# A scan kernel's decays: one PSUM name with two buffers, or two names with one buffer each

## The chip, the cores and the metric

The kernel runs on one core of a Trainium2 chip. The metric is the device time of one execution in microseconds (us), lower is better. A core has five engines that run side by side, each with its own in-order queue: TensorE (PE, matmuls; its weight loads are listed as PEld), VectorE (DVE), ScalarE (ACT), GpSimd (POOL) and SyncE (SP, which here issues transfers). PSUM is the memory that TensorE writes its results to; it has eight banks of 128 partitions x 512 float32, and this kernel also uses it as fast scratch space for ScalarE and VectorE.

## The reference

The input is x of shape (2, 256, 64, 64), that is 2 batches of 256 channels by 4096 tokens. Layer 0 is a group norm and one selective scan (a Mamba block with 256 inner channels). Layer 1 is two such scans with 512 inner channels over the normalized tokens, one forward and one backward in time, and then a mixture of 8 experts of three 256 x 256 matrices each. All in float32. The heart of each of the six scans (three for each batch) is

```python
dA = jnp.exp(dt[..., None] * A)                        # decay, 16 states per channel
dBu = dt[..., None] * Bm[:, :, None, :] * xs[..., None]  # input
# h[t] = dA[t] * h[t-1] + dBu[t]
y = jnp.einsum('blds,bls->bld', hs, Cm) + xs * Dvec
y = y * jax.nn.silu(z)
return y @ out_proj_w.T
```

## The kernel before

**Tiles and loops.** Each scan is cut into 8 chunks of T = 512 tokens. A (scan, chunk) is a *step*; 48 steps run one after the other. A step with 256 inner channels has 8 *quads*, one with 512 has 16. A quad is 128 partitions x 4 groups x 512 tokens; the partitions hold 32 channels x 4 states, so that a quad is a share of the 16 states of 128 channels. There are 640 quads, numbered g. Each is worked in two *halves* h = 0 and h = 1 of two groups each; a half is a *slot*, 2g + h, of 1280 in all. The position of a quad in its run of eight is n.

**The work of one half.**
- `emit_b` (L742, GpSimd, for the whole quad, some quads ahead): the input dBu into an SBUF tile bq, from rxdt and bc.
- `emit_join` (L763, ScalarE): adds the carried state to the first token of the second group.
- `emit_decay` (L752, ScalarE, two instructions of 128 x 512): exp(dt * A) into a PSUM tile da of two banks. It calls `emit_join` first.
- `emit_scan` (L778, VectorE, 128 x 1024): the recurrence over both groups. It reads da and bq. Its result replaces da, or, where `on_pool` says so, bq.
- For a half whose result is in da: `emit_times_c` (L787, VectorE) multiplies by C into bq, and `emit_carry` (L797, ScalarE) copies the last token into h_state. For quads with n of 0, 2 or 5, and every second time for the first half of n = 4, the result goes to bq and GpSimd does both (L802, L803); then the scan is the last reader of da.
- `emit_sum` (L811, TensorE): adds over the states into y; L824 (VectorE) multiplies by the gate.

**Order.** The loop over slots writes the order of every engine out by hand: at slot s come, on ScalarE, the carry of half s-1, then the decay of half s+1, then other ScalarE work that is due; on VectorE the scan of half s, then other work, then its product with C. `in_order()` ties each engine to that order. The other work, placed by a table of slots (`SLOTS`, `Slots`), is what the next steps need: input projection, conv and its tanh (L531, L540, L544), softplus (L589 to L591 on ScalarE, L594 on VectorE, L598 on GpSimd), gates (L621, L624), norms (L399 to L431), the output projection (L841, L843, L858), and matmuls of the experts (L992, L1005) in TensorE's gaps. Behind the last slot, from about 4470 us, come the experts that found no place (L1326, L1330, L1350) and their weighting and summing (L1275, L1337, L1356).

**PSUM.** In the scan part the pools take all eight banks: `psp` three banks for projections, conv, norms and experts (L191), `ps_y` one for y, `ps_d` four for da, two tiles of two banks each (L201). Pools hand their buffers to tiles when the program is built: a tile that asks for a name (tag) gets one of the buffers of that name, and its first writer waits for the last user of the tile that had the buffer before.

Of the kernel before, what the change touches and what calls it, by code (L numbers as in the profile page):

```python
# [42 lines left out]
F32 = mybir.dt.float32  # L43
# [4 lines left out]
P = 128  # L48
NB, C, L = 2, 256, 4096
KC = C // P  # L50
T = 512
# [85 lines left out]
def hybrid_kernel(ctx: ExitStack, tc: tile.TileContext, a: dict, out: bass.AP):  # L137
    nc = tc.nc
    PSUM = bass.MemoryType.PSUM
# [54 lines left out]
    with ExitStack() as st:  # L194
# [3 lines left out]
        bcd = st.enter_context(tc.tile_pool(name="bcd", bufs=2, space=DRAM))  # L198
        bqp = st.enter_context(tc.tile_pool(name="bqp", bufs=6))
        ps_y = st.enter_context(tc.tile_pool(name="ps_y", bufs=1, space=PSUM))  # L200
        ps_d = st.enter_context(tc.tile_pool(name="ps_d", bufs=2, space=PSUM))  # L201

        lngb = const.tile([P, 2, KC], F32, name="lngb")
        one_row = const.tile([P, 1], F32, name="one_row")
# [464 lines left out]
        bq, da, y = {}, {}, {}  # L669
        pending, wanted = [], []  # L670

        def at(g):

            i, jp, n = quads[g]
            return i, 2 * jp + n // SG, n % SG
# [68 lines left out]
        def emit_decay(g, h):  # L744
            if g >= nq or ("rdt", at(g)[1]) not in cks[at(g)[0]]:
                return
            emit_join(g, h)
            i, j, sg = at(g)
            da[g, h] = ps_d.tile([P, 2, T], F32, tag="da", name=f"da_{g}_{h}")
            for k in range(2):  # L750
                q = 2 * h + k
                nc.scalar.activation(  # L752
                    da[g, h][:, k, :], cks[i]["rdt", j][:, q, :], AF.Exp,
                    scale=steps[i][0].w["a"][:, j, q * SG + sg : q * SG + sg + 1],
                )

        def emit_join(g, h):

            i, j, sg = at(g)
            job, c = steps[i]  # L760
            q = 2 * h + 1
            if c:
                nc.scalar.activation(  # L763
                    bq[g][:, q, 0:1], job.h[:, j, sg, q : q + 1], AF.Identity,
                    scale=cks[i]["a0", j][:, h, sg : sg + 1], bias=bq[g][:, q, 0:1],
                )
# [332 lines left out]
        flush(0)  # L1099
        want_b(0, 1, 2)  # L1100
        emit_decay(0, 0)

        in_order()
        done = []
        for g in range(nq):
            i, jp, n = quads[g]
            for h in range(2):
# [14 lines left out]
                if slot:  # L1122
                    emit_carry(*divmod(slot - 1, 2))
                emit_decay(*divmod(slot + 1, 2))
                sl.run(slot, "act")

# [27 lines left out]
    with ExitStack() as st:  # L1154
# [166 lines left out]
        def layer(x, l, e, tag):  # L1321
            h = mk.tile([P, KC, T], F32, tag=f"h{l}", name=f"h{l}_{tag}", bufs=2 + 2 * l)
            for m in range(KC):
                ps = psp.tile([P, T], F32, tag="ps", name=f"hp{l}_{tag}_{m}")
                for k in range(KC):
                    nc.tensor.matmul(  # L1326
                        ps, we[f"W{l + 1}", e][:, k, m * P : (m + 1) * P], x[:, k, :],
                        start=(k == 0), stop=(k == KC - 1),
                    )
                nc.scalar.activation(  # L1330
                    h[:, m, :], ps, AF.Relu,
                    bias=of[:, l, e, m : m + 1], scale=sc[:, l, e, m : m + 1],
                )
            return h
# [104 lines left out]
        for at, (b, i, e) in enumerate(pairs):  # L1439
# [5 lines left out]
            h = layer(n[b, i], 0, e, f"{i}_{e}_{b}")  # L1445
# [15 lines left out]
            while ahead and spent < target and ahead[0][2] in wb:  # L1461
                cost, fn, _ = ahead.pop(0)
# [119 lines left out]
```

## Time and profile before

| what | value |
|---|---|
| time, median of 3 runs | 5000.81 us (5000.21 to 5005.29) |
| profiled execution, its own time | 5004.36 us |
| profiled execution, span of its instructions | 5002.6 us |
| mean granted TensorE clock | 0.928 of full |
| VectorE busy in the span | 4568.5 us |
| GpSimd busy in the span | 4342.2 us |
| ScalarE busy in the span | 3617.3 us |
| TensorE busy in the span | 4256.4 us |
| decays (L752) | 2560 instructions, 686 ns each |
| scans (L778) | 1280 instructions, 2.28 to 2.35 us each |

Busy time is what an engine spent on instructions; the page also gives it as a digit (tenths) for each of 40 equal slices of the span. A row of waits reads "engine tile line <- engine tile line: us in total, times, longest us": the first waited for the second. A row of the timeline reads "start, duration, engine, line, operation, out<-in", and in brackets the idle time of the engine just before it and what ended it.

### The profile page before, as it was taken

Reading aid. Unit: us, or ns where it says so; the run is one execution under the profiler, and the core shown is the slowest. Engines: PE = TensorE matmul, PEld = TensorE weight load, DVE = VectorE, ACT = ScalarE, POOL = GpSimd, SP = SyncE. Lnnn points to the kernel's source line nnn. Section 1 sums busy time; section 2 is a strip of 40 time slices with the busy share of each in tenths; the row PEclk is TensorE's granted clock in tenths of the full one; section 3 lists DMA queues with packets and bytes.
Section 4 is the critical chain, followed back from the end, with each engine's and each line's share of the span. In section 5 each row is a group of like instructions: output and inputs, shape, how many; then the busy total and the mean of one; then the engine's idle time right before and its main releaser. Section 6 shows DMA issues by size and latency. Waiting matters only on the chain. (4 is left out here: it accounts for less than half of the span.)

```text
span 5002.6 us, 47346 instructions
## 1 busy us (share of the span) xinstructions
PE 4256.4 (85%) x14912; PEld 1473.8 (29%) x14912; DVE 4568.5 (91%) x3097; ACT 3617.3 (72%) x7304; POOL 4342.2 (87%) x1424
## 2 busy tenths in 40 slices
PE   5777778778776899989999999889868999989999
PEld 1222222222222233333333333223222333334444
DVE  6998999999999999999999999999999999964655
ACT  5777777777777788877788788888767888862232
POOL 6998999999999999999999999999999999960000
PEclk8778899999887999999999999999989999999999
DMA  5455454444444555446776555555434455436643
GB/s 192 157 188 168 157 168 153 157 144 154 163 158 148 175 179 176 166 171 232 246 238 216 171 174 169 189 171 189 169 127 146 171 185 191 171 121 236 227 160 126
DMA packets 335408, 875.26 MB, mean 175 GB/s; under 512 B 36315, under 2 KB 111861, under 8 KB 293173
## 3 DMA queue, kind: packets, MB, share of 16 engines
q1 hardware_dynamic: 326164, 835.39, 48.3%
q0 software_dynamic: 8992, 36.85, 2.8%
q8 instruction: 118, 1.93, 0.2%
q14 instruction: 134, 1.09, 0.1%
HBM read 673.27 MB, written 198.84 MB: 174 GB/s over the span
## 5 line engine op out<-in xcount | busy, mean ns | idle before, releaser
L742 POOL TENSOR_TENSOR bq<-rxdt,bc 128x2048 f32<-128x2048 f32 x640 | 2894.3, 4545 | 15.7 <-DMA rxdt<-xdtd 7.7
L752 ACT ACTIVATE da<-rdt,w_a 128x512 f32<-128x512 f32 x2560 | 1756.9, 686 | 114.2 <-DVE bq L778 68.0
L778 DVE TENSOR_TENSOR_SCAN da<-da,h_state,bq 128x1024 f32<-128x1024 f32 x664 | 1558.0, 2346 | 60.4 <-ACT da L752 46.2
L803 POOL TENSOR_TENSOR bq<-bq,bc 128x2048 f32<-128x2048 f32 (+1 forms) x280 | 1180.4, 4216 | 22.6
L778 DVE TENSOR_TENSOR_SCAN bq<-da,h_state,bq 128x1024 f32<-128x1024 f32 x456 | 1059.7, 2338 | 22.0 <-ACT da L752 21.8
L811 PE MATMUL y<-bq,stack 128*32 128x512 f32 x5120 | 744.8, 667 | 254.3 <-POOL bq L803 229.5
L787 DVE TENSOR_TENSOR bq<-da,bc 128x1024 f32<-128x1024 f32 x760 | 926.4, 1219 | 15.7
L992 PE MATMUL e<-eh,ew 128*128 128x512 f32 x1376 | 669.8, 621 | 52.3 <-DVE sp L594 13.6
L797 ACT COPY h_state<-da 128x2 f32<-128x2 f32 x759 | 119.3, 157 | 631.6 <-DVE bq L787 628.3
L763 ACT ACTIVATE bq<-h_state,bq,a 128x1 f32<-128x1 f32 x1120 | 429.8, 384 | 2.9 <-POOL bq L742 2.3
L992 PEld LDWEIGHTS e<-eh,ew 128*128 128x128 f32 x1376 | 250.5, 194 | 466.5 <-issue 234.9
L458 PE MATMUL z<-nx,w_in 128*128 128x512 f32 x640 | 326.6, 639 | 62.5 <-DVE q L423 21.1
L811 PEld LDWEIGHTS y<-bq,stack 128*32 128x32 f32 x5120 | 140.7, 116 | 798.8 <-POOL bq L803 347.7
L531 PE MATMUL conv<-xs,w_conv 64*64 64x512 f32 x2560 | 346.6, 617 | 31.3 <-ACT xs L515 29.1
L992 PE MATMUL e<-en,ew 128*128 128x512 f32 x688 | 329.6, 612 | 26.9 <-DVE xr L891 16.1
L458 PE MATMUL xs<-nx,w_in 128*128 128x512 f32 x640 | 316.9, 622 | 34.7 <-DVE sz L624 20.7
L1330 ACT ACTIVATE h<-hp,of,sc 128x512 f32<-128x512 f32 x168 | 130.6, 778 | 277.5 <-PE hp L1326 274.7
L1005 ACT ACTIVATE eh<-e,of,sc 128x512 f32<-128x512 f32 x344 | 260.1, 769 | 53.9 <-PE e L992 53.6
L843 PE MATMUL o<-sz,w_out 128*128 128x512 f32 x640 | 295.7, 601 | 0.0
L598 POOL TENSOR_TENSOR xdt<-sp,xc 128x512 f32<-128x512 f32 x160 | 203.3, 1274 | 49.7 <-DVE sp L594 49.7
L778 DVE TENSOR_TENSOR_SCAN da<-da,bq 128x1024 f32<-128x1024 f32 x96 | 219.4, 2286 | 4.3 <-ACT da L752 2.3
L458 PEld LDWEIGHTS z<-nx,w_in 128*128 128x128 f32 x640 | 123.6, 202 | 266.3 <-issue 146.8
(145 smaller groups left out, 4762.3 us busy)
## 6 DMA issues: line engine op xcount, KB each, us to landing
rxdt<-xdtd SPq DMA_DIRECT2D x160, 1024.0 KB, 6.1
rdt<-dtd SPq DMA_DIRECT2D x160, 1024.0 KB, 6.8
bc<-bcd SPq DMA_DIRECT2D x384, 256.0 KB, 3.2
ew<-in_W SPq DMA_DIRECT2D x172, 256.0 KB, 4.5
u<-u SPq DMA_DIRECT2D x86, 512.0 KB, 5.7
u<-eu SPq DMA_DIRECT2D x82, 512.0 KB, 4.1
dtd<-sp SPq DMA_DIRECT2D x160, 256.0 KB, 3.3
xdtd<-xdt SPq DMA_DIRECT2D x160, 256.0 KB, 3.5
```

The costliest lines, as they stand in the source:

```text
L458: nc.tensor.matmul(ps, job.matrices["in", half][:, k, j * P : (j + 1) * P], rhs, start=(k == 0), stop=(k == KC - 1),)
L531: nc.tensor.matmul(v[r][64 * col : 64 * col + 64, :], job.matrices["conv"][rows, 2 * jp + j, k, :], ck["xs", jp][rows, j, k : k + T] if k ...
L742: nc.gpsimd.tensor_tensor(bq[g], ck["rxdt", j], over_groups(ck["bc", 0, sg]), ALU.mult)
L752: nc.scalar.activation(da[g, h][:, k, :], cks[i]["rdt", j][:, q, :], AF.Exp, scale=steps[i][0].w["a"][:, j, q * SG + sg : q * SG + sg + 1],)
L763: nc.scalar.activation(bq[g][:, q, 0:1], job.h[:, j, sg, q : q + 1], AF.Identity, scale=cks[i]["a0", j][:, h, sg : sg + 1], bias=bq[g][:, ...
L778: nc.vector.tensor_tensor_scan(b if on_pool(g, h) else d, d, b, job.h[:, j, sg, 2 * h : 2 * h + 1] if c else 0.0, ALU.mult, ALU.add,)
L787: nc.vector.tensor_tensor(bq[g][:, two, :], d, cks[i]["bc", 1, sg].rearrange("p (o t) -> p o t", o=1).to_broadcast([P, 2, T]), ALU.mult,)
L803: nc.gpsimd.tensor_tensor(b, b, cks[i]["bc", 1, sg].rearrange("p (o t) -> p o t", o=1).to_broadcast([P, groups, T]), ALU.mult,)
L811: nc.tensor.matmul(y[i, j][q * CG : (q + 1) * CG, :], stack, bq[g][:, q, :], start=False, stop=(sg == SG - 1),)
L843: nc.tensor.matmul(v[m], job.w["out"][:, j, m * P : (m + 1) * P], ck["sz", j], start=False, stop=(j == job.nj - 1),)
L992: nc.tensor.matmul(ps, ew[l][:, k, m * P : (m + 1) * P], key[x][:, k, :], start=(k == 0), stop=(k == KC - 1),)
L1005: nc.scalar.activation(key[dst][:, m, :], key["ps", l, m], AF.Relu, bias=of[:, l, e, m : m + 1], scale=sc[:, l, e, m : m + 1],)
```

## The change

The pool of the decays gets one buffer for each name in place of two, and the two halves of a quad get names of their own, da0 and da1. Each name has one pair of banks; the pool keeps four banks. First halves then always lie in one pair and second halves in the other.

```diff
-        ps_d = st.enter_context(tc.tile_pool(name="ps_d", bufs=2, space=PSUM))
+        ps_d = st.enter_context(tc.tile_pool(name="ps_d", bufs=1, space=PSUM))
...
-            da[g, h] = ps_d.tile([P, 2, T], F32, tag="da", name=f"da_{g}_{h}")
+            da[g, h] = ps_d.tile([P, 2, T], F32, tag=f"da{h}", name=f"da_{g}_{h}")
```

## The prediction

> **What bounds the kernel now.** I read the page's busy rows and slices first, then the waits of each engine between 60 and 4467 us (first to last scan), then the timeline around single decays.
>
> ```profile
> PE 4256.4 (85%) x14912; PEld 1473.8 (29%) x14912; DVE 4568.5 (91%) x3097; ACT 3617.3 (72%) x7304; POOL 4342.2 (87%) x1424
> DVE  6998999999999999999999999999999999964655
> POOL 6998999999999999999999999999999999960000
> ```
>
> From the second to about the 36th slice (to some 4470 us) the scans run, and there VectorE and GpSimd are both at 9 tenths; ScalarE never is. The rest (533 us) is expert matmuls behind the scans. By stretch (columns: us, PE, PEld, DVE, ACT, POOL busy with counts, clock, DMA share, GB/s):
>
> ```profile
> 1000.00:1500.00 500.00, 394.25 (x1559) 119.72 (x1552) 482.92 (x331) 379.84 (x797) 485.78 (x160) 0.90 0.46 154
> 1500.00:2000.00 500.00, 424.12 (x1569) 141.27 (x1568) 491.81 (x320) 390.91 (x808) 497.34 (x161) 0.93 0.49 170
> 2000.00:2500.00 500.00, 458.68 (x1505) 166.29 (x1503) 478.96 (x288) 398.45 (x802) 489.18 (x149) 0.96 0.58 203
> ```
>
> Neither leads everywhere. In the first and third row both leave 10 to 21 us idle; in the second GpSimd leaves 2.7 us and VectorE 8.2. Who waits for whom (us, times, longest; 60 to 4467 us):
>
> ```profile
> DVE da L778 <- ACT da L752: 48.4, 55, 3.9
> DVE bq L778 <- ACT da L752: 26.3, 22, 2.2
> DVE da L778 <- POOL h_state L802: 2.6, 3, 1.6
> DVE da L778 <- POOL bq L742: 1.2, 1, 1.2
> POOL h_state L802 <- DVE bq L778: 53.3, 37, 5.7
> ACT da L752 <- DVE bq L778: 68.0, 80, 2.0
> ```
>
> VectorE's largest idle time, 74.7 us, is scans waiting for their decays. For GpSimd it waits about 4 us in all; GpSimd waits 53.3 us for its scans. So VectorE mostly sets the pace with GpSimd close behind, and decays cost it 74.7 us. The last row is the change's subject: 80 decays waited for a scan of the kind that leaves its result in bq. Which scan? Here is one (start, duration, engine, line):
>
> ```profile
> 1054.35 1.21 DVE L787 TENSOR_TENSOR bq<-da,bc 128x1024 f32<-128x1024 f32 x1
> 1055.48 2.34 DVE L778 TENSOR_TENSOR_SCAN bq<-da,h_state,bq 128x1024 f32<-128x1024 f32 x1
> 1057.74 0.67 DVE L594 SCALAR_TENSOR_TENSOR sp<-dt,sp 128x512 f32<-128x512 f32 x1
> 1059.30 2.36 DVE L778 TENSOR_TENSOR_SCAN da<-da,h_state,bq 128x1024 f32<-128x1024 f32 x1 [0.90 <-ACT da L752]
> ```
>
> and ScalarE beside it:
>
> ```profile
> 1055.81 0.14 ACT L797 COPY h_state<-da 128x2 f32<-128x2 f32 x1
> 1055.85 0.39 ACT L763 ACTIVATE bq<-h_state,bq,a 128x1 f32<-128x1 f32 x1
> 1057.85 1.42 ACT L752 ACTIVATE da<-rdt,w_a 128x512 f32<-128x512 f32 x2 [1.62 <-DVE bq L778]
> ```
>
> The decay at 1057.85 feeds the scan at 1059.30. The half two before it was finished with its banks at 1055.95 (the carry copy, L797), yet the decay stood until 1057.82, where the scan of the half *just before* ended. Nothing but a da pair is shared by those two instructions. So the two pairs do not strictly alternate: this half was given its neighbour's pair while the other stood empty.
>
> **The change part by part.** It adds and removes no instruction, transfer or bank: ps_d stays at four banks, two pairs. The order on every engine is the program's own. Decays are emitted h = 0, 1, 0, 1, so with a pair for each h, half s can only wait for half s-2, never for s-1.
>
> *The waits that go.* Following all 1280 decay pairs through the timeline, I count 31 that start within 0.15 us of the end of the immediately preceding scan and whose idle time that scan ended: 43.4 us of ScalarE. (The other waits of the 80 end with the scan two back, as they must, and stay.) What VectorE loses is the idle time ahead of the decay's scan. In 11 of the 31 it is 1.48 us (two decays of 0.69 and the hand-over), in 13 it is 0.90 (one 0.67 us instruction stood between), in one 0.81, and in six nothing, as filler covered it. Sum: 11 x 1.48 + 13 x 0.90 + 0.81 = 28.8 us.
>
> After the change, the decay of the example could start at about 1056.2, behind its join (L763), and end near 1057.6. The softplus step (L594) ends at 1058.41 and the scan would follow. ScalarE's work behind the decay (L589 to L591) moves up by 1.6 us as well; what is late next on VectorE is then nothing but its own queue.
>
> *What is added.* Behind a half that took its neighbour's pair, the next half used to find a pair idle since three halves back; now it waits for the one two back. That costs ScalarE nothing new, because it has already passed the same scan in its own order. I put it at 0. Its bounds: 0, and in each of the 31 places the hand-over seen above between the scan's end and the decay, 0.03 us, together 1 us. Queued behind such a decay on ScalarE would be the evictions of conv, z and the experts, for which PE and VectorE wait.
>
> *A rule of the Trainium skill.* The row: a 0.90 us bubble in every step from 716 to 1398 us, at the same place. Perfetto Trace Analysis, section Optimization Strategy, says that a gap repeating on the engine that should be saturated can mean too little SBUF or PSUM for the next tile, and it names buffer count and tile size. By that reading this change would bring 0, as it adds no bank, and a third pair would be wanted. The trace goes the other way: a pair was empty from 1055.95 while the decay waited. What lacked was the choice, not the count. I side with the trace.
>
> *How much of the 28.8 us reaches the end.* A gain of VectorE counts only where GpSimd was waiting for VectorE afterwards; where GpSimd runs without a wait, it absorbs the gain. From the waits in order of time (GpSimd's at L802 and L598):
> - 60 to 500 us: five gaps, 4.5 us; GpSimd waits about 13 us. Some of this stretch is limited at job changes by PE and ScalarE (3.5 us on thx at 441): I count 3.4.
> - 500 to 1500: seven gaps, 6.3 us; a step of 113 us has about 0.97 + 0.98 us of GpSimd waits, enough for 0.90, but also 0.2 and 0.63 us of VectorE waiting for the conv's tanh, which may grow: 5.0.
> - 1500 to 2220: 0.90 + 1.48. GpSimd waits nowhere between 1487 and 2277, and at 2220.88 VectorE waits 1.19 us for GpSimd: 0.
> - 2220 to 2830: five of 1.48 and one of 0.81, 8.2 us; GpSimd waits some 19 us, but VectorE also has waits of 2.9, 2.7 and 3.9 us for late decays that have other causes: 6.5.
> - 2830 to 3560: 1.48 at 3508, followed by GpSimd waits of 0.69 and 1.48: 1.5.
> - 3560 to 4400: 1.48 at 3832, no GpSimd wait until 4429: 0.
> - 4400 to 4460: three of 1.48; GpSimd then waits 5.7 us: 4.4.
>
> Sum 20.8 us. Behind it, PE's sum of the last quad (L811 at 4468.14) follows the last scan and PE runs without a gap until 4494, so the tail moves with it. Against the profiled execution (5004.36 us, of which 1.8 lie outside its span of 5002.6) that is 4983.6; against the median of the runs, 5000.81, it is 4980.0, the number I give.
>
> **The rivals.**
> *The gain is absorbed.* GpSimd is 97 to 99% busy; if it is the true pace-maker in more than the two stretches, only the places directly ahead of its waits count. For it: the 1500 to 2000 row. Against it: 53.3 us of waits for scans. With the last stretch (4.4), half of the fourth (3.3) and 1.5, it is 9 us: 4992. Should the pairs alternate already, so that the change does nothing, it is 5001; the example speaks against it.
>
> *More comes back.* ScalarE gets 43.4 us of standing back, and other late decays (74.7 - 28.8 = 45.9 us) have a late ScalarE behind them. All 28.8 and a quarter of 45.9: 40 us, 4961.
>
> *Slower: other banks are dealt anew.* The mechanism that dealt da pairs badly also deals the three banks of psp (L191) and the three th buffers, by when tiles are held to be free. If the releases of da move, those choices may move too. A bad choice there makes PE wait for an eviction, then ScalarE for PE, then a decay is late. The price is that of the nearest row, 0.90 us on VectorE for each. It decides where more than 23 new ones lie on the path (20.8 / 0.90). With one in each of the 48 steps, 43 us are lost and 21 won: +22, 5023. Against it: the order of each engine is fixed and PE has 41 to 106 us idle in the three stretches shown.
>
> **How the numbers follow.** The likeliest case, most of the gain (4972 to 4990), has 0.60. More coming back has 0.12, absorbed or nothing 0.21, newly dealt banks 0.07. About 0.2% (10 us) is what a measurement of this kernel can tell from no change. Absorbed splits around 4991, so that faster by over 0.2% gets 0.60 + 0.12 + 0.03 = 0.75, within 0.2% 0.18, and slower by more 0.07. For the range I leave out the outer half of more coming back (0.06), newly dealt banks (0.07) and the part of absorbed in which nothing at all is won (0.06), 0.19 together: 4965 to 5000.
>
> **What would show it.** In the changed profile: ScalarE's wait of da for DVE bq L778 falls from 68.0 us to about 25, and each such wait that is left ends with a scan two halves back; scans waiting for decays fall from 74.7 to about 46; GpSimd's wait for scans falls by some 20 us; instructions stay at 47346 but for semaphores; the last scan starts near 4444 in place of 4465. It is wrong if decays still wait for the scan just before them, or if these waits go and the last scan stays: then GpSimd set the pace and VectorE's idle time has only changed its name. New waits of PE or ScalarE in rows of conv, e or thx would be the slower case.

## The result, and the profile after

The changed kernel takes 4978.36 us (median of 5, 4972.65 to 4982.88), the kernel before 5000.21 us (median of 5). The ratio is 0.9954, 95% interval [0.9939, 0.9968]: 22 us or somewhat under half a percent faster, twice what the measurement can tell from no change. The forecast was 4980.0, range 4965 to 5000.

The profiled execution of the changed kernel took 4972.65 us, its span 4970.9 us. It is 5.7 us below its median, and the one of before was some 4 us above, so the pair of traces shows 31.7 us where the medians show 22. Of the 31.7 the scans account for 27.8: the last scan starts at 4437.4 us in place of 4465.2. The rest behind it took 533.5 us in place of 537.4. In the other traces below that rest took 533 or 537 to 540 us without any edit to it, so these 3.9 us are not the change's.

The page's busy row: the work is the same to 0.1% on VectorE, ScalarE and GpSimd, and the number of instructions has not changed. TensorE is busy 30.6 us less, at a mean granted clock of 0.933 in place of 0.928; E7 shows a part of it.

```profile
PE 4225.8 (85%) x14912; PEld 1476.1 (30%) x14912; DVE 4567.6 (92%) x3097; ACT 3613.1 (73%) x7304; POOL 4340.4 (87%) x1424
```

Who waits for whom, 60 to 4467 us (us, times, longest):

```profile
DVE da L778 <- ACT da L752: 35.7, 52, 4.9
DVE bq L778 <- ACT da L752: 9.3, 10, 2.2
DVE da L778 <- POOL h_state L802: 4.3, 4, 1.6
POOL h_state L802 <- DVE bq L778: 36.0, 29, 3.1
ACT da L752 <- DVE bq L778: 23.6, 48, 1.4
ACT nx L493 <- DMA x<-in_x: 20.6, 7, 4.2
```

Scans waiting for decays: 74.7 us before, 45.0 now (46 forecast). Decays waiting for a scan: 68.0 before, 23.6 now (25 forecast), and followed one by one through the trace none of these waits ends with the scan just before it; there were 31 such. GpSimd's wait for scans: 53.3 to 36.0. The last row is new: it was 8.6 us, see E4.

The same half as in the prediction's example, first VectorE, then ScalarE:

```profile
1050.28 2.34 DVE L778 TENSOR_TENSOR_SCAN bq<-da,h_state,bq 128x1024 f32<-128x1024 f32 x1
1052.53 0.66 DVE L594 SCALAR_TENSOR_TENSOR sp<-dt,sp 128x512 f32<-128x512 f32 x1
1053.11 2.35 DVE L778 TENSOR_TENSOR_SCAN da<-da,h_state,bq 128x1024 f32<-128x1024 f32 x1
```

```profile
1050.61 0.14 ACT L797 COPY h_state<-da 128x2 f32<-128x2 f32 x1
1050.65 0.39 ACT L763 ACTIVATE bq<-h_state,bq,a 128x1 f32<-128x1 f32 x1
1050.94 1.40 ACT L752 ACTIVATE da<-rdt,w_a 128x512 f32<-128x512 f32 x2
```

The decay at 1050.94 follows its join at once and runs beside the scan that it used to wait for (1050.28 to 1052.62). The scan at 1053.11 follows softplus without a gap; the 0.90 us are gone.

Was anything else dealt anew? The two programs have the same instructions in the same order on every engine. Only decays differ in what they wait for, and no tile but the decays' lies at another place. In the program of before, 37 of the 1280 halves have their neighbour's pair: the 31 that were seen to wait, and six whose decay came late enough. In the changed program none has.

How much earlier the same scan starts in the changed trace gives the gain by stretch:

| stretch of before (us) | forecast gain | measured gain |
|---|---|---|
| 60 to 526 | 3.4 | 0.5 |
| 526 to 1481 | 5.0 | 7.6 |
| 1481 to 2235 | 0 | -0.8 |
| 2235 to 2836 | 6.5 | 11.7 |
| 2836 to 3548 | 1.5 | 0.9 |
| 3548 to 4409 | 0 | 0.7 |
| 4409 to the last scan | 4.4 | 7.2 |
| sum | 20.8 | 27.8 |

The second row is the least certain. In a second trace of the changed kernel (E11) the second scan, 526 us to about 1430, took 897.5 us against 893.2 in the first and 901.3 in the kernel before. So up to 4 us there, and of single scans in that part or behind 2240 us, can belong to the execution and not to an edit; E11's last scan is 1.8 us later than the first trace's, which would make the sum 26. The sum is of the right size, yet most of its terms are off. The experiments ask why.

### The profile page after: what moved, and what is told of

The parts are those of the page before. It is cut to its first block, busy times and chain, and to the rows that moved or that the text cites. A ratio compares the mean times of both kernels' runs of the same rounds, so it can differ in the third digit from the quotient of the medians.

```text
span 4970.9 us, 47346 instructions
## 1 busy us (share of the span) xinstructions
PE 4225.8 (85%) x14912; PEld 1476.1 (30%) x14912; DVE 4567.6 (92%) x3097; ACT 3613.1 (73%) x7304; POOL 4340.4 (87%) x1424
## 5 line engine op out<-in xcount | busy, mean ns | idle before, releaser
L742 POOL TENSOR_TENSOR bq<-rxdt,bc 128x2048 f32<-128x2048 f32 x640 | 2893.8, 4544 | 15.2 <-DMA rxdt<-xdtd 7.3
L752 ACT ACTIVATE da<-rdt,w_a 128x512 f32<-128x512 f32 x2560 | 1756.9, 686 | 70.0 <-DVE bq L778 23.6
L787 DVE TENSOR_TENSOR bq<-da,bc 128x1024 f32<-128x1024 f32 x760 | 926.2, 1219 | 15.7
L992 PE MATMUL e<-eh,ew 128*128 128x512 f32 x1376 | 659.5, 613 | 43.3 <-DVE sp L594 14.4
L531 PE MATMUL conv<-xs,w_conv 64*64 64x512 f32 x2560 | 334.6, 603 | 22.7 <-ACT xs L515 20.4
```

Of the source, the lines that this page charges most:

```text
L531: nc.tensor.matmul(v[r][64 * col : 64 * col + 64, :], job.matrices["conv"][rows, 2 * jp + j, k, :], ck["xs", jp][rows, j, k : k + T] if k ...
L742: nc.gpsimd.tensor_tensor(bq[g], ck["rxdt", j], over_groups(ck["bc", 0, sg]), ALU.mult)
L752: nc.scalar.activation(da[g, h][:, k, :], cks[i]["rdt", j][:, q, :], AF.Exp, scale=steps[i][0].w["a"][:, j, q * SG + sg : q * SG + sg + 1],)
L787: nc.vector.tensor_tensor(bq[g][:, two, :], d, cks[i]["bc", 1, sg].rearrange("p (o t) -> p o t", o=1).to_broadcast([P, 2, T]), ALU.mult,)
L992: nc.tensor.matmul(ps, ew[l][:, k, m * P : (m + 1) * P], key[x][:, k, :], start=(k == 0), stop=(k == KC - 1),)
```

## The experiments

Most of them name the pair by a table in the changed kernel. A half in `shared` gets its neighbour's pair, all others alternate. The table adds four lines, so that decays are L756 and scans L782 there.

```diff
+        pair = [0]
+        for slot in range(1, 2 * nq):
+            pair.append(pair[-1] if slot in shared else 1 - pair[-1])
...
-            da[g, h] = ps_d.tile([P, 2, T], F32, tag=f"da{h}", name=f"da_{g}_{h}")
+            da[g, h] = ps_d.tile([P, 2, T], F32, tag=f"da{pair[2 * g + h]}", name=f"da_{g}_{h}")
```

"Later by" below is the start of a scan in the experiment's trace less that of the same scan in the changed kernel's.

**E1: 13 shared pairs where GpSimd has no waits.**

```diff
+        shared = {437 + 32 * k for k in range(6)} | {1045 + 32 * k for k in range(7)}
```

> The changed kernel, with the pair of banks of each half named by a table: all halves alternate, but 13 (the second half of the second n = 2 quad of a step, whose neighbour leaves its result in bq) are given their neighbour's pair, six between 1500 and 2150 us and seven between 3600 and 4350 us, where the changed kernel's GpSimd has no waits for scans. Theory A (a wrong choice of pair costs VectorE its idle time, and GpSimd's own pace absorbs it here): each of the 13 decays waits for the scan just before it, 1.48 us of idle VectorE each, 19 us in all, but the last scan starts within 5 us of the changed kernel's 4437 us, and the time is 4975 to 4985 us. Rival B (every idle microsecond of VectorE is on the path): the last scan starts near 4456 and the time is about 4997 us.

Measured: 4988.43 us, ratio to before 0.9977 [0.9969, 0.9985]. All 13 decays wait for the scan just before them, and each leaves VectorE 1.48 us idle. One of them:

```profile
1925.32 2.35 DVE L782 TENSOR_TENSOR_SCAN bq<-da,h_state,bq 128x1024 f32<-128x1024 f32 x1 [1.48 <-ACT da L756]
```

The last scan starts 15.3 us late (4452.7; 13.5 against E11's trace), 10 us more than theory A allowed. The first pair of each set (1597 and 3658 us) costs nothing: within some 60 us, waits that VectorE has in the changed kernel are shorter by as much. The five pairs that follow in the third scan raise the delay from 1.85 us at 1689 us to 3.44, 4.69, 5.66, 6.86 and 7.96 us at 2175 us: 1.0 to 1.6 each, and nothing comes back within the step. At 2220 us 2.2 us do come back, in a wait of 2.16 us that the changed kernel has there anyway; 3.2 us are lost anew from 2235 to 2280 us, where no pair is shared (1.7 of them at a wait like the last one of E7). Busy time from 1600 to 2190 us in the changed kernel, then in E1 (columns as in the prediction):

```profile
1600.00:2190.00 590.00, 526.29 (x1916) 182.67 (x1920) 583.33 (x379) 477.48 (x986) 586.86 (x189) 0.97 0.51 179
```

```profile
1600.00:2190.00 590.00, 528.58 (x1903) 179.18 (x1902) 578.66 (x377) 476.91 (x985) 583.30 (x186) 0.95 0.49 176
```

GpSimd's idle time grows from 3.1 to 6.7 us. It set the pace there, but with VectorE so close behind that it absorbs only some 0.3 us of each 1.48 of these five. Neither A nor B holds as written; B is nearer.

**E2: 13 shared pairs where GpSimd waits.**

```diff
+        shared = {149 + 32 * k for k in range(7)} | {629} | {645 + 16 * k for k in range(5)}
```

> The same table, with the 13 shared pairs where the changed kernel's GpSimd waits for scans: seven between 590 and 1300 us (one in each step of the second scan), six between 2240 and 2520 us. Theory A: the 19 us of VectorE's idle time come through but for what lies beside other waits, the last scan starts 13 to 19 us later than 4437 us and the time is 4990 to 4998 us. Rival B: the same 19 us, as in the other place. Rival C (the gain of the change came from something else than the shared pairs): no difference in either, 4978 us.

Measured: 4988.50 us, 0.9978 [0.9971, 0.9985]; the last scan 14.7 us late. The seven of the second scan cost 11.5 us against the first trace of the changed kernel, some 7 against E11's (1.0 to 1.6 each), the six behind 2240 us 4.7 us (0.8 each). In the time there is no difference between E1's place and this one. So C falls, 13 shared pairs in either place bring back half of the 22 us; and the map of GpSimd's waits alone, by which the prediction weighed each stretch, is no guide to the price.

**E3: 240 shared pairs.**

```diff
+        shared = {16 * k + n for k in range(nq // 8) for n in (1, 5, 11)}
```

> The same table, with every second half of an n = 0, 2 or 5 quad in its neighbour's pair: 240 of 1280 instead of the 31 that were seen to wait before the change. Theory A: up to 1.48 us each, 355 us, less what GpSimd's pace and filler absorb, some 20 to 100 us: 5230 to 5310 us. A lower price, below 0.5 us each (under 5100 us), would mean that the decay is seldom on the path and that the gain of 22 us is owed to a few places only.

Measured: 5333.79 us, 1.0673 [1.0657, 1.0689], above the expected band. Totals of waits of ScalarE and of GpSimd:

```profile
ACT da L756 <- DVE bq L782: 420.7, 248, 2.7
```

```profile
POOL h_state L806 <- DVE bq L782: 341.3, 118, 6.9
```

231 of the 240 decays are seen to wait for the scan just before them. VectorE's gaps at their scans are 242 us, but the last scan starts 363 us late: 1.5 us for each shared pair, half as much again as the gaps at their own scans. What the rest is made of was not isolated; TensorE's mean granted clock is 0.91 here, and 0.93 in the changed kernel.

**E4: the scaling of x one slot later.** After the change ScalarE stands 20.6 us at L493 for a transfer, since it is earlier and the transfer is not.

```diff
-AHEAD_SLOTS = dict(x=-7, scale=-5, xs=(-1, 0), conv=(2,), dbc=10, dt=(14, 22), z=(-4, 12))
+AHEAD_SLOTS = dict(x=-7, scale=-4, xs=(-1, 0), conv=(2,), dbc=10, dt=(14, 22), z=(-3, 12))
```

> The changed kernel, with the scaling of the next batch's x (L493) moved one slot later, and the first gate behind it too: in eight steps ScalarE stands 2.4 to 4.2 us at L493 for the transfer of x, and in five of them the scan behind the decay waits 0.3 to 3.6 us, 8.4 us in all. If late decays of any cause are on the path while GpSimd waits for scans, ScalarE's wait for in_x goes from 20.6 us to under 2, and the last scan starts 4 to 8 us earlier: about 4972 us. If GpSimd absorbs it, the waits go and the time stays at 4978 us.

Measured: 4976.98 us, 0.9955 [0.9938, 0.9972], not to be told from the changed kernel. The wait falls to 4.0 us, and the last two steps of the second scan take 219.9 us in place of 226.2; between 2280 and 2820 us 4.9 us are lost again. The two traces of the changed kernel take the same time for that stretch to 0.3 us, though single scans within it differ by up to 4. The execution that was traced here was the slowest of the four (4984.75 us), so whether the edit costs those 4.9 us is not shown. No better version.

**E6: shared pairs in the first scan, and the three at the end.**

```diff
+        shared = {16 * k + 5 for k in range(1, 8)} | {1265, 1269, 1273}
```

> The table with ten shared pairs: seven in the first scan (60 to 480 us, one in each step of 55 us) and the three at the very end that the kernel before had (4375, 4389 and 4403 us). In the first scan five such pairs of before cost 0.5 us and not the 4.5 us of their gaps. Theory A1 (a step of 8 quads gives a delay back, because GpSimd's copy of the state, L802, or the sums of its products are what ends last there): the seven cost under 2 us at slot 128. Theory A2 (before's five just stood in lucky places): they cost 7 x 1.1 = 8 us. For the three at the end: the loss of before, 7.2 us, comes back in full if they are its whole cause; 4.4 us if the rest was something else.

Measured: 5002.45 us, 1.001 [0.9999, 1.002]. The three at the end cost 7.24 us, exactly what before lost there. In the first scan A1 falls: the five pairs whose decay waits for the neighbour's scan cost 10.3 us, 2.1 each (gaps of 0.9 at their scans, 0.63 at the next scan in four of the five, and longer waits for TensorE and GpSimd behind them). The sixth waits for nothing and costs nothing. The seventh costs 9.0 us. It stands ahead of the second batch's group norm. ScalarE's queue there:

```profile
490.56 1.42 ACT L756 ACTIVATE da<-rdt,w_a 128x512 f32<-128x512 f32 x2 [1.81 <-DVE bq L782]
...
506.49 0.26 ACT L183 ACTIVATE gn_s<-gm,columns 128x2 f32<-128x2 f32 x1 [10.26 <-PE gm L337]
```

ScalarE then stands 10.26 us at the head of its queue for a small matmul, with decays behind it. That matmul waits for VectorE, where two instructions on 128 x 2 elements take 3.50 and 4.42 us. In the changed kernel they take 0.29 and 0.16. VectorE, then GpSimd beside it:

```profile
497.86 3.50 DVE L335 TENSOR_TENSOR dm<-dm 128x2 f32<-128x2 f32 x1
501.39 4.42 DVE L336 TENSOR_TENSOR dm<-dm,mv 128x2 f32<-128x2 f32 x1
```

```profile
496.82 4.52 POOL L807 TENSOR_TENSOR bq<-bq,bc 128x2048 f32<-128x2048 f32 x1
501.30 4.50 POOL L746 TENSOR_TENSOR bq<-rxdt,bc 128x2048 f32<-128x2048 f32 x1
```

Each of the two ends within 0.02 us of a product of GpSimd (501.36 and 501.34, 505.81 and 505.80). In the changed kernel both start (487.34, 487.66) just before that product does (487.82); here they come behind its start. The gap of 1.49 us and the 7.47 us by which the two are longer make up the 9.0 us. The last section comes back to this.

So before's five cost 0.5 us by their places, and the stretch is not insensitive. Compared scan by scan, VectorE's waits behind those five, most of them for TensorE and GpSimd, are some 4 us longer in the changed kernel than in the kernel before: the delay fell into waits that were there anyway.

**E7: three shared pairs near 2230 us alone; E5: the middle one of each cluster alone.**

```diff
+        shared = {625, 629, 633}      # E7
+        shared = {629, 1269}          # E5
```

> The table with three shared pairs alone, near 2230, 2245 and 2259 us, as the kernel before had them. Before lost 7.2 us there against the changed kernel though VectorE's gaps at the three scans were 4.45 us. If a late ScalarE carries each delay on to the next decays (the chain), the last scan starts 7 us later than the changed kernel's at slot 640 and some of it stays to the end; if the excess was chance, 4.4 us.

> The table with two shared pairs, each the middle one of the two clusters of three (near 2245 and 4389 us). Each cluster of three cost 7.0 to 7.25 us against gaps of 4.45. Theory D (a delay is carried on: a decay that is late pushes ScalarE's queue, and the next shared pair in reach adds to it): alone each costs 1.5 us or less, together under 3 us at the end. Theory E (each place has its price of 2.4 us whatever stands around it): 2.4 us each.

Measured: E7 4981.28 us, 0.9961 [0.9945, 0.9977]; E5 4977.40 us, 0.9958 [0.9943, 0.9974]. In E7 the scans at 2280 us are 7.0 us later than those at 2228; in E5 each of the two costs 0.92 us. VectorE in E7, with its waits, and in E5:

```profile
2233.77 2.35 DVE L782 TENSOR_TENSOR_SCAN bq<-da,h_state,bq 128x1024 f32<-128x1024 f32 x1 [1.48 <-ACT da L756]
2236.77 2.36 DVE L782 TENSOR_TENSOR_SCAN da<-da,h_state,bq 128x1024 f32<-128x1024 f32 x1 [0.65 <-ACT da L756]
2248.10 2.35 DVE L782 TENSOR_TENSOR_SCAN bq<-da,h_state,bq 128x1024 f32<-128x1024 f32 x1 [1.48 <-ACT da L756]
2262.36 2.36 DVE L782 TENSOR_TENSOR_SCAN da<-da,h_state,bq 128x1024 f32<-128x1024 f32 x1 [1.48 <-ACT da L756]
2270.16 2.35 DVE L782 TENSOR_TENSOR_SCAN bq<-da,h_state,bq 128x1024 f32<-128x1024 f32 x1 [0.22 <-ACT da L756]
2278.68 2.36 DVE L782 TENSOR_TENSOR_SCAN da<-da,h_state,bq 128x1024 f32<-128x1024 f32 x1 [2.67 <-ACT da L756]
```

```profile
2244.67 2.35 DVE L782 TENSOR_TENSOR_SCAN bq<-da,h_state,bq 128x1024 f32<-128x1024 f32 x1 [1.49 <-ACT da L756]
2271.11 2.36 DVE L782 TENSOR_TENSOR_SCAN da<-da,h_state,bq 128x1024 f32<-128x1024 f32 x1 [0.41 <-ACT da L756]
```

The last row of E7 shares no pair, and yet waits 2.67 us. Its decay is late because ScalarE is:

```profile
2276.29 0.78 ACT L1009 ACTIVATE eh<-e,of,sc 128x512 f32<-128x512 f32 x1 [1.70 <-PE e L996]
2276.97 0.37 ACT L767 ACTIVATE bq<-h_state,bq,a 128x1 f32<-128x1 f32 x1
2277.25 1.40 ACT L756 ACTIVATE da<-rdt,w_a 128x512 f32<-128x512 f32 x2
```

In E5 the corresponding wait is 0.41 us, in the changed kernel 0.42. The prices are those of theory D: alone a shared pair costs less than its gap (0.92 of 1.48), three within 30 us cost 7.0 us at gaps of 4.45. Its reason is only half right, for what the three delays add up to is idle time of TensorE. TensorE in E7, and then the stretch behind its wait, in E7 and at the same instructions in E5 (columns as in the prediction):

```profile
2270.00 6.26 PE L996 MATMUL e<-eh,ew 128*128 128x512 f32 x8 [4.90 <-DVE xr L895]
```

```profile
2270.00:2275.60 5.60, 5.60 (x7) 2.37 (x8) 5.41 (x3) 3.66 (x7) 4.54 (x3) 0.54 0.93 282
```

```profile
2264.90:2270.50 5.60, 5.54 (x13) 2.58 (x14) 5.57 (x4) 5.09 (x10) 5.52 (x4) 1.00 0.54 184
```

The matmul waits 4.90 us for an instruction of the late VectorE (2.20 us in the changed kernel, 3.12 in E5). Behind that wait TensorE's granted clock is 0.54 and it gets through 7 matmuls, where E5 has 1.00 and 13. So ScalarE's two evictions wait for TensorE (0.90 and 1.70 us), and the decay behind them is late. The same stands in the kernel before at both clusters and in E6 at the last one: 4.90 us of idle TensorE, 6.8 us at half clock from the last 1.1 to 1.6 us of it on, then a scan that waits 2.86 to 2.93 us. That the idle time alone decides is not shown: after 2.20 us most traces show full clock at these places, but E1, E4 and E8 show 3.4 us at half clock at one of them.

**E8 and E9: which engine sets the pace.** E8 leaves out one product of GpSimd in each of 15 steps, E9 one of VectorE.

```diff
+            if 8 <= i < 23 and j == 2 and sg == 2:             # E8, in emit_times_c_quad, ahead of L803's product
+                return
+            if 8 <= i < 23 and j == 2 and (sg, h) == (3, 1):   # E9, in emit_times_c
+                return
```

> The changed kernel without one of GpSimd's products with C (L803, 4.5 us) in each of 15 steps from the second scan's first step to the third scan's last but one (530 to 2190 us); what those products feed is not the reference's. If GpSimd sets the pace where it has no waits (1500 to 2150 us), each of those seven steps gets shorter, by up to VectorE's own slack of 1 to 2 us, and those before it by less; if VectorE with its decays sets the pace everywhere, no step changes by more than 0.3 us.

> The changed kernel without one of VectorE's products with C (L787, 1.22 us) in each of the same 15 steps; what those products feed is not the reference's. If VectorE sets the pace, each step gets shorter by about 1.2 us, 18 us in all; if GpSimd does from 1500 us on, those steps change by less than 0.3 us each, and only the second scan's (530 to 1420 us) gain, 8 to 9 us in all.

Measured: E8 4965.08 us, 0.9931 [0.9908, 0.9953]; E9 4979.22 us, 0.9959 [0.9940, 0.9979]. E8's third-scan steps get 0.35 to 0.6 us shorter each between 1690 and 2175 us, for 4.5 us of GpSimd less; the step from 1525 to 1635 us gets 2.5 us shorter, more than was expected. In the second scan nothing moves in the steps up to about 1190 us (668.6 us for six steps, 667.0 and 669.9 in the two traces of the changed kernel); the last two are 6.6 us shorter, much as in E4; in both the long waits at L493 (4.2 and 4.1 us in the changed kernel) are shorter, here 0.0 us. E9 moves nothing in either scan (666.9 us for those six steps; 485.5 in four and a half of the third, 485.6 in the changed kernel). GpSimd's waits from 1530 to 2190 us in E8 (there are none in the changed kernel), then VectorE's from 530 to 1420 us in E9:

```profile
POOL h_state L802 <- DVE bq L778: 19.1, 16, 1.5
```

```profile
DVE da L778 <- ACT da L752: 16.5, 12, 4.5
```

In E8 VectorE sets the pace after 0.35 to 0.6 us: that is how far GpSimd was ahead as the bound, and it is close to what E1's pairs had absorbed. In E9 the 1.22 us of a product turned into waits for decays (8.4 us in the changed kernel, 16.5 here): the product that was left out covered a decay. So in the second scan it is neither engine's work but the chain from decay to scan that ends last.

**E10: a third place for decays, in SBUF.**

```diff
+        sb_d = st.enter_context(tc.tile_pool(name="sb_d", bufs=1))
...
-            da[g, h] = ps_d.tile([P, 2, T], F32, tag=f"da{h}", name=f"da_{g}_{h}")
+            slot = 2 * g + h
+            home, pair = (sb_d, "sb") if slot % 3 == 2 else (ps_d, slot % 3)
+            da[g, h] = home.tile([P, 2, T], F32, tag=f"da{pair}", name=f"da_{g}_{h}")
```

> The changed kernel with a third place for decays: every third half lies in an SBUF tile (4 KB for each partition), the other two in the two pairs of banks. This tests whether the count of places binds once the choice is right. If it does, the 48 waits of decays for a scan two halves back (23.6 us of ScalarE) go, scans wait less for decays (45 us now) and the last scan starts up to 10 us earlier. If it does not, the waits go and nothing else moves. The place may cost something by itself: the scans and products that read two SBUF operands may take longer, or GpSimd's may; if they do, by 5% of a scan, that is 427 x 0.12 = 50 us on VectorE, 5030 us.

Measured: 6280.30 us, 1.2559 [1.2538, 1.2580]. Groups of VectorE and of GpSimd in E10 (count, busy us, mean ns):

```profile
L790 DVE TENSOR_TENSOR bq<-da,bc 128x1024 f32<-128x1024 f32 x760 | 1724.7, 2269 | 15.6
```

```profile
L743 POOL TENSOR_TENSOR bq<-rxdt,bc 128x2048 f32<-128x2048 f32 x640 | 3446.2, 5403 | 34.4 <-issue 16.7 <-PE y L814 8.4 <-DMA rxdt<-xdtd 7.4
```

and in the changed kernel:

```profile
L787 DVE TENSOR_TENSOR bq<-da,bc 128x1024 f32<-128x1024 f32 x760 | 926.2, 1219 | 15.7
```

```profile
L742 POOL TENSOR_TENSOR bq<-rxdt,bc 128x2048 f32<-128x2048 f32 x640 | 2893.8, 4544 | 15.2 <-DMA rxdt<-xdtd 7.3 <-issue 7.3 <-PE y L811 0.6
```

The place costs so much that the run says nothing on the count. Whether a third pair of PSUM banks would help stays open: all eight banks are taken.

**E11: the changed kernel again.**

> The changed kernel once more, for a second trace: to see which of the 31.7 us between the two profiled executions is the change's and which differs from one execution to the next. If the scans are repeatable, the last scan starts within 2 us of 4437; the rest behind it took 537.4 us before and 533.5 us after, and 537 is expected in about half of the executions.

Measured: 4974.81 us, 0.9950 [0.9935, 0.9965]. Its last scan starts 1.8 us later than in the first trace, and the rest takes 533.5 us again.

## Why the prediction was right

**The cause was right.** The prediction read from one wait that two neighbouring halves shared a pair while the other stood empty. E1 and E2 put that back by name, 13 times each, and each brought the idle time of 1.48 us and about 10 us of the time; E6 gave back before's loss at the end to 0.01 us. The slower rival, other banks dealt anew, is out: no other tile moved.

**The gaps, 28.8 us, were right as a count.** All 31 waits went, and scans' waiting for decays fell by 29.7 us.

**The step that failed is the weighing by stretch**, "A gain of VectorE counts only where GpSimd was waiting for VectorE afterwards". E1 shows that a GpSimd without waits absorbed some 0.3 us for most pairs, not 1.48, and E2 that the place made no difference to the time. What did absorb delays in full was a wait of VectorE itself, for whatever engine, that stood behind them. Two terms came out near nought for before (1481 to 2235, 3548 to 4409), but not for that reason alone: in the first, before's two delays did come through (it falls behind by 1.2 us from 1481 to 1698); 1.0 us of it was worked off over the three steps behind, 0.3 to 0.4 us in each, and another 1.0 us at 2220 us, in the wait that the prediction names.

**The mis-sized terms.** The clusters: two times 4.45 us of gaps were counted at or below their gaps and were 7.2 each: TensorE at half clock behind the third delay made a fourth wait of 2.9 us, of which 0.4 is left after the change (E7 against E5). The prediction had read the first of these, the 2.9 us between 2220 and 2830 us, as having another cause, and it put nothing for TensorE's clock. This is the rival "more comes back" in two places. The first scan: 3.4 forecast, 0.5 measured, as before's five stood where the delay was hidden; E6 shows that others cost 2.1. The second scan: 7.6 in place of 5.0, but only 3.7 against E11's trace, so this term is not shown to be wrong. The errors up and down left a total that is near by some luck: 20.8 forecast, 27.8 between two traces, 22 between the medians.

**What was not seen.** ScalarE, once earlier, waits for the transfer at L493: 8.6 to 20.6 us. The prediction named nothing that a ScalarE in advance would meet. E4 shows that mending it brings nothing that can be measured.

**The rule of the Trainium skill.** Perfetto Trace Analysis, section Optimization Strategy, says that a repeated bubble *can* mean too few or too small buffers. Here it did not: the choice of pair removed the bubble of 0.90 us at the same count of banks. That a higher count would not bring more is not shown.

## What to carry to other kernels

Where two buffers serve two alternating users, look at *which* earlier user ends a wait: the one two back is double buffering, the neighbour means that the pool dealt the wrong buffer, and names of their own cured that here without another bank. Count the gaps ahead of the bound engine for the size, but expect a factor between 0 and 2 or more on each: here a gap alone cost 0.6 of itself, three in a row 1.6, one ahead of two small instructions 6. So look at what the delay moves: a wait that is there anyway takes it in, an idle TensorE may come back at half clock, an instruction may fall behind another engine's. An engine without waits is not therefore slack for another's delay: leave a little of its work out and see how soon the next bound appears.

## What the runs showed of the hardware

E10 was the surprise: every third decay in SBUF in place of PSUM made the kernel 26% slower, with nothing else edited. VectorE's products rose from 1219 to 2269 ns on average and up to 5392 (1226 at most before the edit), its scans from about 2340 to between 2760 and 2830 on average, and GpSimd's products from 4544 to 5403. The trace shows the shape that the Trainium skill describes (SBUF — State Buffer, section Who interferes with whom): a VectorE instruction with two SBUF inputs contends with a GpSimd instruction that reads SBUF. With da in PSUM both scan and product have one full-length SBUF input, and none of the 760 products took longer than 1226 ns beside a GpSimd that was busy 97% of the time. The expected 5% of a scan was far too low. E6 shows how long such a wait can be: its two small instructions (L335, L336) have both inputs in SBUF, and the second took 4.42 us in place of 0.16, until GpSimd's 4.50 us were over.

The second is TensorE's clock. Where three shared pairs follow one another (twice in the kernel before, once each in E6 and E7), the traces show 4.90 us of idle TensorE and 6.8 us at half clock, most of them behind the wait (granted 0.50 to 0.54 there). The changed kernel shows 2.20 us of idle and full clock there, in both of its traces. Each cluster was dearer by 2.2 to 2.5 us for it, on VectorE, though TensorE is not what bounds this part of the kernel.
